# A graph layer on one core: which batches SyncE fetches, how far ahead rows and features are asked for, and where recomputed batches lie

## The chip, the cores and the metric

One core of a Trainium2 chip runs the kernel in one launch. Its engines are TensorE (PE: matmuls; PEld its weight loads), VectorE (DVE), ScalarE (ACT), GpSimd (POOL) and SyncE (SP), which here only issues DMAs. All of it is float32. The metric is device time in microseconds: the median of three runs before is 3925.41 us (3924.81 to 3928.84). A separate profiled execution took 3917.68 us.

## The reference

A layer of a graph network with scalar and vector features on 12500 nodes and 400000 edges, sorted by target node. The number of edges of a node falls along the list, since targets are drawn as 12500 u².

```python
h = relu(layernorm(x))                       # 12500 x 160: 64 scalars, 32 vectors of 3
s = [h0 @ W_sc0, h1 @ W_sc1] * a             # self-connection, a: one number a node
y = [h0 @ W_l1_0, h1 @ W_l1_1] * a           # what a node sends
w = silu(edge_attr_16 @ fc_W1) @ fc_W2       # 192 weights an edge, from 16 features
ys = y[src]                                  # 400000 rows of 160: the gather
mid = products of w, ys and edge_attr_4      # per edge, 96 scalars and 96 vectors
z = zeros.at[dst].add(mid)                   # sum over the edges of a node
out = x + C_S * s + C_X * [z0 @ W_l2_0, z1 @ W_l2_1] * a
```

## The kernel before

**Node stage** (to about 100 us). 98 tiles of 128 nodes are loaded, normalized, transposed and mapped to y, which is stored to a table y_d in HBM, a row of 640 bytes a node. GpSimd uses this time for 72 early fetches of rows of x (L378).

**Edge loop.** The 400000 edges are 3125 tiles of 128, in 782 batches of four tiles. For a batch b the steps are:

- `features` (L393): SyncE loads the edge features, 8 batches in one block `xe`, two DMAs a block.
- `hidden` (L630) and `activate`: TensorE and ScalarE make the hidden layer for two batches.
- `weigh` (L651): the 192 weights of each edge, four matmuls, into `pw`.
- `gather` (L603): GpSimd issues one indirect DMA a tile, 128 rows of y_d into `yg`. Two of a batch's four are issued half a batch later in the loop. An added dependency makes the gathers of batch b + AHEAD wait for the sums of batch b.
- `products` (L561 and L565, the helper `multiply`): VectorE multiplies weights by gathered rows into `pr`; it also makes the selection matrix `sel` (L665, L667).
- `sums` (L681): TensorE multiplies `sel` by `pr` and so adds edges into windows of 32 nodes. A window takes 24 tiles at the start and 3 at the end, four windows are a group; VectorE turns each finished window (L687, L688), and `linear` (L694), `add` (L706) and `accumulate` (L717) bring a group into the output.

Not all batches are gathered by GpSimd:

- **Recomputed batches** (`x_batch`, 18 of them): their rows of x were fetched in the node stage, so y is computed again on the spot. The four rows of a lane lie in slot u of `xr`. The steps are `hot`, `hot_turn` (L776), `look_up` (L788), `pick`, `x_center`, `x_turn` (L803, L804), `x_map` (L816, L817), spread over 16 batches. Before, these batches lie 16 apart: 19, 35, ... 291.
- **Batches that SyncE fetches** (`row_batch`, 12 of them): SyncE reads 16 places from a table `ri` into registers (L618) and issues 16 transfers of one row each (L623), 32 times for a batch. Before, they lie 64 apart: 72, 136, ... 776, and sixteen rows are asked for every two batches. Their rows go into slots of `xr` that are no longer needed.

The **self-connection** is computed in 49 pairs of node tiles (`skip_load` at L727, `skip_turn` L741 and L742, `skip_map` L751 and L752, `skip_add`), a pair every nine batches; before, from batch 296 to 736.

Other work of a block of 24 batches: SyncE loads its four edge numbers, sources and targets (L401, L403, L405) and stores the targets' places in windows (L419), and VectorE computes these (`relate`).

The order is written out by hand: each engine runs its instructions in the order of the Python loop, and waits only for data, for a free buffer or for the added dependencies. `AHEAD = 4`, `EARLY = 8`, `SB = 16` (spacing of recomputed batches), `RB = 64` (spacing of SyncE's batches).

Of the kernel before, what the change touches and what calls it, by code (L numbers as in the profile page):

```python
# [10 lines left out]
F32 = mybir.dt.float32  # L11
# [8 lines left out]
P = 128  # L20
M0 = 64
M1 = 32
D = M0 + 3 * M1
# [6 lines left out]
GT = 4  # L30
# [6 lines left out]
MW = BLK // WTS[-1]  # L37
GN = 8
HN = 2
AHEAD = 4  # L40
EARLY = 8
SB = 16
LATE = 8
XB = 18
SK = 9
RB = 64
RN = 16
LO = D - P
EPS = 1e-5
# [5 lines left out]
def kernel(  # L55
# [19 lines left out]
    nc = tc.nc  # L75
# [47 lines left out]
    GE = NG - LATE  # L123
# [20 lines left out]

    ygp = ctx.enter_context(tc.tile_pool(name="yg", bufs=6))
    ld = ctx.enter_context(tc.tile_pool(name="ld", bufs=2))
    evp = ctx.enter_context(tc.tile_pool(name="ev", bufs=2))
    rp = ctx.enter_context(tc.tile_pool(name="rel", bufs=2))
    RF = RB + 8
    NR = (NB - 1 - RF) // RB + 1  # L150
    RP = 4
    assert NR - 1 <= XB and RP * NR <= P
    ri = const.tile([RP * NR, P // RP * GT], I32, name="ri")
    rg = const.tile([P, GT, D], F32, name="rg")
    blocks, ev4, lows = {}, {}, {}

    before = ctx.enter_context(ExitStack())
# [105 lines left out]
    def row_index():  # L263
        t = row_batch(0) * GT
        for i in range(NR):
            t = row_batch(i) * GT
            nc.sync.dma_start(ri[RP * i:RP * (i + 1), :].rearrange("q (p k) -> q p k", k=GT),
                              src[:, t:t + GT].rearrange("(q p) k -> q p k", q=RP))

    def row_place():  # L270
        nc.vector.tensor_scalar(ri, ri, float(D * 4), None, ALU.mult)
# [86 lines left out]

    def x_batch(u):

        return SB * (u + 1) + 3

    def x_index(us):
        t = x_batch(0) * GT
        every = src[:, t:t + XB * SB * GT].rearrange("p (u r) -> p u r", r=SB * GT)[:, :, 0:GT]
        nc.sync.dma_start(xi[:, us, :], every[:, us, :])

    def x_split():

# [16 lines left out]
    def features(b):  # L386
        blk = b * GT // BT
        if blk not in blocks:

            xe = ld.tile([P, 512], F32, name="xe")  # L390
            v = e16[blk * P:(blk + 1) * P, :].rearrange("(s k f) (h c) -> k s (f h) c", s=4, k=2, h=2)
            for k in range(2):
                nc.sync.dma_start(xe[:, 256 * k:256 * (k + 1)], v[k])  # L393
            blocks[blk] = xe
# [30 lines left out]
    with (  # L425
# [81 lines left out]
        for i, (g, n) in enumerate(groups[:LEAD]):  # L507
            load_x(g, n)
            if i == 1:
                x_index(slice(2, XB))  # L510
                nc.sync.dma_start(a_sb, attr)
        last = len(steps) - 1
        more = list(groups[LEAD:])
# [1 line left out]
        for q in range(len(steps) + 7):  # L515
            if q <= last and steps[q][2] == 0 and more:
                load_x(*more.pop(0))
            for f in range(XB * GT * q // (last + 6), min(XB * GT * (q + 1) // (last + 6), XB * GT)):
                x_fetch(f, mapped.get(q - 6))
            if q == 8:  # L520
                e4_load(0)
            if q == 10:
                row_index()
            for load in loads[2 * q - 24:2 * q - 22] if q >= 12 else []:
                load()
            if q == 24:
                for b in range(min(EARLY, NB)):
                    features(b)
            if q == 16:
                rows_of_windows()  # L530
                lowest(0)
            if q == 18:
                pt = nd_ph.tile([MW, P], F32, name="ph")[:windows_in(0), :]
                turn_low(0, pt)
                most(0, pt)
            if q == 22:
                spread(0, nd_ph.tile([P, MW], F32, name="ph")[:, :windows_in(0)])
            for stage, lag in ((scales, 3), (leave, 7), (out_of_psum, 4), (roots, 2), (turn_rows, 3), (map_rows, 5),
                               (moments, 0), (center, 1)):
                if 0 <= q - lag <= last:  # L540
                    stage(q - lag)
            if q == 2:
                node_weights()
            if q == last + 3:
                nc.vector.tensor_scalar(nm, mv[:, :, 0], -1.0, None, ALU.mult)
                x_split()
                edge_weights()
                relate(rp, 0)
                row_place()
        assert 12 + len(loads) // 2 <= last and x_batch(XB) <= NB  # L550
    before.close()


# [14 lines left out]
    with (  # L568
# [43 lines left out]
        def row_fetch(i, n):  # L612

            b = row_batch(i)
            if n == 0:
                rows[b] = xr[:, i - 1, :, :] if i else rg
            q, o = divmod(n * RN, P // RP * GT)
            _, at_row = nc.values_load_multi_w_load_instructions(  # L618
                ri[RP * i + q:RP * i + q + 1, o:o + RN], engines=[mybir.EngineType.SP], min_val=0, max_val=(N - 1) * D * 4,
                skip_runtime_bounds_check_because="places of nodes, as the indices of the other fetches")  # L620
            for m, v in enumerate(at_row):
                e, k = divmod(n * RN + m, GT)
                nc.sync.dma_start(rows[b].bitcast(U8)[e:e + 1, k, :], y_b[ds(v, D * 4)].unsqueeze(0))  # L623
# [218 lines left out]
        def extras(b):  # L842

            g = group_of[b]
            k = b - first_of[g]
            q, r = divmod(b, KB)
            u, v = divmod(b, SB)
            su, sv = divmod(b - SS, SK)
            if b % 2 == 0 and b + 4 < NB:
                s = (b + 4) // 2  # L850
                activate(s, hidden(s))
            if g and k == 0:
                linear(g - 1)
# [24 lines left out]
            if u < XB and v in (3, 6):  # L878
                left(None)
                picked = look_up(u, HN * (v == 6))  # L880
                waiting[-1] = lambda: pick(u, HN * (v == 6), *picked)
            if r == KB - 6 and q + 2 == NQ:
                left(None)
                cnt = p_x.tile([1, 1], F32, name="px")
                any_far(cnt)
                waiting[-1] = lambda: far_flag(cnt)
            if r == KB - 13 and q + 1 < NQ:
                left(None)
                low_pt = p_x.tile([MW, P], F32, name="px")[:windows_in(q + 1), :]
                turn_low(q + 1, low_pt)  # L890
                waiting[-1] = lambda: most(q + 1, low_pt)
# [12 lines left out]
        for b in range(NB):  # L904
            g = group_of[b]
            k = b - first_of[g]
            if b + EARLY < NB:
                features(b + EARLY)
            q, r = divmod(b, KB)
            if r == 0:  # L910
                e4_load(q + 1)
            if r == KB - 4:
                e4_join(q + 1)
            u, v = divmod(b, SB)
            su, sv = divmod(b - SS, SK)
# [29 lines left out]
        assert SS + NU * SK <= first_of[GE] + K and NQ > 1  # L945
# [162 lines left out]
```

## Time and profile before

| what | before |
|---|---|
| median of three runs | 3925.41 us |
| profiled execution | 3917.68 us, span 3915.5 us |
| busy: TensorE, GpSimd, VectorE, ScalarE | 3586.6, 2917.6, 2748.4, 623.6 us |
| gathers from y_d on GpSimd | 3005, 947 ns each |
| row transfers on SyncE | 6144 |
| mean granted TensorE clock | 0.97 |
| data moved by DMA | 329.82 MB, mean 84 GB/s |

The span runs from the first to the last instruction, and the profiled execution's time holds 2.2 us more. A group of instructions is one line of the code: engine, operation, output<-inputs, count | busy us, mean ns of one | idle us of that engine just before them, and what ended most of it ("issue": nothing that the profile shows). A timeline's row is start, length, engine, line; in brackets the idle time before it. A table of stretches gives for each stretch its length, and the busy time and count of TensorE's matmuls, its weight loads, VectorE, ScalarE and GpSimd, then TensorE's granted clock, the mean share of the DMA engines and GB/s. SPq is SyncE's queue of DMA issues.

### The profile page before, as it was taken

The page shows a single profiled execution, that of the slowest core. Times are in us where ns is not written, and L with a number is a line of the kernel's source. Part 1 is how long each engine was busy: PE and PEld are TensorE (multiplying, and loading weights), DVE is VectorE, ACT ScalarE, POOL GpSimd, SP SyncE. Part 2 cuts the span into 40 slices and gives each one's busy share as a digit, 9 for nine tenths or more (in the row PEclk, how much of TensorE's full clock was granted, in tenths as well). Part 3 has the DMA queues.
Part 4 walks back from the last instruction along what each step waited for, and adds up shares of the span by engine and source line. Part 5 has one row for each costly group of instructions (what it writes and reads, how often), then busy time and mean ns, then how long its engine had stood idle before and what let it go on. Part 6 is the DMA issues. An engine that isn't in the chain of part 4 may idle for free.

```text
span 3915.5 us, 66013 instructions
## 1 busy us (share of the span) xinstructions
PE 3586.6 (92%) x17274; PEld 2321.5 (59%) x17274; DVE 2748.4 (70%) x6899; ACT 623.6 (16%) x1863; POOL 2917.6 (75%) x3085
## 2 busy tenths in 40 slices
PE   7898999999999999889999999989899999999988
PEld 7555555555656655555555565555566666666555
DVE  7566666666667666666677677777677777778776
ACT  6111111111111111111111111111111111111111
POOL 6777777777777777777777777777777777777775
PEclk8899999999999999999999999999999999999999
DMA  8333333323333232333333333333333333333324
GB/s 233 78 79 76 78 78 76 77 73 78 77 75 78 74 80 75 83 83 80 80 82 77 84 79 82 80 80 79 82 80 83 80 79 82 83 80 79 79 74 135
DMA packets 262773, 329.82 MB, mean 84 GB/s; under 512 B 78472, under 2 KB 213160, under 8 KB 262392
## 3 DMA queue, kind: packets, MB, share of 16 engines
q0 software_dynamic: 147696, 252.26, 26.2%
q1 hardware_dynamic: 114072, 73.01, 6.7%
q8 instruction: 140, 2.29, 0.2%
q14 instruction: 241, 1.97, 0.2%
q10 hardware_dynamic: 624, 0.27, 0.0%
HBM read 307.70 MB, written 17.61 MB: 83 GB/s over the span
## 4 chain that ended last, share of the span: by engine, by line
PE 42%; DMA 20%; DVE 18%; issue 11%; POOL 8%; DVEq 1%; SPq 0%; ACT 0%; POOLq 0%; ACTq 0%
PE pz L681 22%; DMA yg<-y_d,src_q 19%; POOL yg L603 8%; PE pw L651 8%; DVE pr L565 7%; PE px L630 5%; DVE pr L561 4%; PE px L694 3%; PE px L706 1%; DVE za L687 1%; DVE at L226 1%; DVE za L688 1%; DVE acc L717 1%; DVE own L665 0%; PE po L485 0%
## 5 line engine op out<-in xcount | busy, mean ns | idle before, releaser
L603 POOL DMA_INDIRECT yg<-y_d,src_q x3005 | 2847.2, 947 | 945.9 <-issue 658.2
L681 PE MATMUL pz<-pr,sel 128*128 128x320 f32 x6250 | 1965.7, 459 | 14.8 <-DVE za L688 14.7
L681 PEld LDWEIGHTS pz<-pr,sel 128*128 128x128 f32 x6250 | 1162.6, 196 | 597.9 <-issue 231.1
L561 DVE TENSOR_TENSOR pr<-pw,yg 128x512 f32<-128x512 f32 x752 | 517.9, 689 | 800.4 <-DMA yg<-y_d,src_q 799.2
L651 PE MATMUL pw<-w,hT 64*128 64x192 f32 x6250 | 737.4, 354 | 252.5 <-DVE pr L565 236.1
L651 PEld LDWEIGHTS pw<-w,hT 64*128 64x128 f32 x6250 | 506.1, 189 | 535.4 <-issue 396.8
L565 DVE TENSOR_TENSOR pr<-pw,yg 128x384 f32<-128x384 f32 x1504 | 760.7, 547 | 0.0
L667 DVE TENSOR_TENSOR sel<-own,pw 128x512 f32<-128x512 f32 x782 | 537.0, 687 | 27.0
L630 PE MATMUL px<-xe,w 32*128 32x512 f32 x782 | 437.3, 640 | 8.8 <-DVE acc L717 7.1
L635 ACT ACTIVATE hT<-px 128x512 f32<-128x512 f32 x391 | 233.4, 597 | 1297.1 <-PE px L630 1292.8
L556 ACT ACTIVATE pw<-ev 128x20 f32<-128x20 f32 x782 | 149.3, 191 | 1417.1 <-PE pw L651 1201.8
L687 DVE STREAM_TRANSPOSE za<-pz 128x160 f32<-128x160 f32 x598 | 203.8, 341 | 233.7 <-PE pz L681 232.8
L694 PEld LDWEIGHTS px<-wo,za 128*128 128x128 f32 x1500 | 211.5, 191 | 106.6 <-issue 68.0
L694 PE MATMUL px<-wo,za 128*128 128x160 f32 x1500 | 243.0, 309 | 8.8 <-DVE high L193 4.3
L630 PEld LDWEIGHTS px<-xe,w 32*128 32x128 f32 x782 | 114.2, 183 | 185.0 <-issue 173.3
L688 DVE STREAM_TRANSPOSE za<-pz 32x160 f32<-32x160 f32 x598 | 201.7, 337 | 20.4
L665 DVE TENSOR_TENSOR own<-iota,pw 128x128 f32<-128x128 f32 x782 | 198.4, 254 | 18.3 <-ACT pw L556 14.7
L706 PE MATMUL px<-os,place 128*128 128x160 f32 x600 | 112.0, 309 | 8.3 <-DVE place L698 3.6
L717 DVE SCALAR_TENSOR_TENSOR acc<-px,a_sb,acc 128x160 f32 x300 | 113.8, 379 | 7.5 <-PE px L706 1.5
L706 PEld LDWEIGHTS px<-os,place 128*128 128x128 f32 x600 | 90.7, 190 | 38.5 <-issue 19.7
L378 POOL DMA_INDIRECT xr<-in_x,xi x72 | 69.2, 962 | 29.2 <-PE po L485 13.7
L696 ACT ACTIVATE os<-px 128x160 f32<-128x160 f32 x150 | 45.6, 304 | 229.6 <-PE px L694 228.6
(131 smaller groups left out, 1380.1 us busy)
## 6 DMA issues: line engine op xcount, KB each, us to landing
xr<-y_d SPq DMA_DIRECT2D x5632, 0.6 KB
yg<-y_d,src_q POOLq DMA_INDIRECT x3005
xe<-in_e SPq DMA_DIRECT2D x196, 128.0 KB
rg<-y_d SPq DMA_DIRECT2D x512, 0.6 KB
xs<-in_x SPq DMA_DIRECT2D x48, 160.0 KB
acc<-in_x SPq DMA_DIRECT2D x11, 640.0 KB
y_d<-ys SPq DMA_DIRECT2D x11, 640.0 KB
out<-acc SPq DMA_DIRECT2D x11, 640.0 KB
```

Source lines behind the costliest of these rows:

```text
L561: nc.vector.tensor_mul(pr[:, :n, :].rearrange("p t (x u) -> p t x u", x=2)[:, :, :, 0:M0], wt[:, :n, 0:NW].rearrange("p t (x u) -> p t x u ...
L565: nc.vector.tensor_mul(pr[:, :n, D * x + M0:D * (x + 1)].rearrange("p t (c u) -> p t c u", c=3), wt[:, :n, 96 * x + M0:96 * (x + 1)].unsqu ...
L603: fetch = nc.gpsimd.indirect_dma_start(out=yg[:, slot(t), :], out_offset=None, in_=y_d, in_offset=bass.IndirectOffsetOnAxis(ap=ev4[t // BL ...
L630: nc.tensor.matmul(ph, w1[r, :], xe[r, :], start=True, stop=True)
L635: nc.scalar.activation(hT, ph, AF.Silu, scale=1.0 / math.sqrt(FC_IN))
L651: nc.tensor.matmul(pw[:, k, 0:NW], hT[r, o:o + P], w2[r, :], start=True, stop=True)
L667: nc.vector.tensor_tensor(sel, own[:, :n, :].unsqueeze(2).to_broadcast([P, n, 4, WN]), wt[:, :n, NW:NW + 4].unsqueeze(3).to_broadcast([P, ...
L681: mm = nc.tensor.matmul(pz[:, 0:PC], sel[:, slot(t), :, :], pr[:, slot(t), :], start=o == 0, stop=last)
L687: nc.vector.transpose(zT[g][:, :, at_w], pz[:, D:PC].rearrange("p (k u) -> p k u", k=ZK))
L688: nc.vector.transpose(zT[g][0:32, :, at_w], pz[0:32, 0:D].rearrange("p (k u) -> p k u", k=ZK))
L694: nc.tensor.matmul(po[:m, :], za[:, k, :m], wo[:, k, :], start=k == 0, stop=k == ZK - 1)
L706: nc.tensor.matmul(ps[:, h, :], place[:m, h, :], os[:m, :], start=True, stop=True)
```

## The change

SyncE's batches become 15, 49 apart (80, 129, ... 766), and sixteen of their rows are asked for every 49 x 16/512 = 1.53 batches, from batch 24 on; each is fully asked for seven batches before its use. They all lie in slots of `xr`, and the separate buffer `rg` goes. Recomputed batches are 43 apart (19, 62, ... 750). Of each 43 batches the first 16 hold the steps of one recomputed batch, and the other 27 hold three pairs of the self-connection, which so runs from batch 16 to about 712. Gathers run six batches ahead of the sums (AHEAD), out of the same six `yg` buffers. Features are asked for 16 batches ahead (EARLY) and have three buffers in a pool of their own. The table of places is loaded at the start of the edge loop (15 loads) and scaled in batch 2, both in the node stage before; the last recomputed batch's index gets a load of its own.

```diff
-AHEAD = 4
-EARLY = 8
+AHEAD = 6
+EARLY = 16
 SB = 16
+PER = 43
...
-RB = 64
+RB = 49
+RS = 24
...
+    fe = ctx.enter_context(tc.tile_pool(name="fe", bufs=3))
...
-    RF = RB + 8
+    RF = RS + RB + 7
     NR = (NB - 1 - RF) // RB + 1
...
-    rg = const.tile([P, GT, D], F32, name="rg")
...
     def x_batch(u):
-        return SB * (u + 1) + 3
+        return PER * u + SB + 3
...
+    def x_index_last():
+        t = x_batch(XB - 1) * GT
+        nc.sync.dma_start(xi[:, XB - 1, :], src[:, t:t + GT])
...
-            xe = ld.tile([P, 512], F32, name="xe")
+            xe = fe.tile([P, 512], F32, name="xe")
...
-            if q == 10:
-                row_index()
...
-                row_place()
...
             if n == 0:
-                rows[b] = xr[:, i - 1, :, :] if i else rg
+                rows[b] = xr[:, i, :, :]
...
-        SS, MAP = SB * XB + 8, 7
+        PAIRS, MAP = (PER - SB) // SK, 7
...
+        def skip_of(b):
+            u, v = divmod(b, PER)
+            if v < SB:
+                return -1, -1
+            return PAIRS * u + (v - SB) // SK, (v - SB) % SK
...
-            u, v = divmod(b, SB)
-            su, sv = divmod(b - SS, SK)
+            u, v = divmod(b, PER)
+            su, sv = skip_of(b)
...
-            if b == SS - 8:
+            if b == SB - 8:
                 skip_load(0)
...
-            if v == 1 and 0 < u <= XB:
-                x_map(u - 1, HN)
+            if v == SB + 1 and u < XB:
+                x_map(u, HN)
...
+            if b == 0:
+                row_index()
...
+            if b == 2:
+                row_place()
-            if v == SB - 2 and u < XB:
+            if v == SB and u < XB:
                 x_scale(u)
...
-            while chunks and chunks[0][0] * RB + chunks[0][1] * RB * RN // (P * GT) <= b:
+            while chunks and RS + chunks[0][0] * RB + chunks[0][1] * RB * RN // (P * GT) <= b:
                 row_fetch(*chunks.pop(0))
```

SyncE's queue early in the edge loop, from one load of a feature block (`xe`) to the next, eight batches later: `TENSOR_LOAD ri` reads sixteen places into registers, and the rows behind it are the transfers of sixteen rows from `y_d`. Before:

```order
64 L393 DMA xe<-in_e 128x1x256 x2
65 L618 TENSOR_LOAD ri
66 L623 DMA rg<-y_d 1x640 x16
67 L618 TENSOR_LOAD ri
68 L623 DMA rg<-y_d 1x640 x16
69 L618 TENSOR_LOAD ri
70 L623 DMA rg<-y_d 1x640 x16
71 L618 TENSOR_LOAD ri
72 L623 DMA rg<-y_d 1x640 x16
73 L393 DMA xe<-in_e 128x1x256 x2
```

and now, with the next feature load as the last row:

```order
79 L622 TENSOR_LOAD ri
80 L627 DMA xr<-y_d 1x640 x16
81 L731 DMA xs<-in_x 128x2x160
82 L622 TENSOR_LOAD ri
83 L627 DMA xr<-y_d 1x640 x16
84 L622 TENSOR_LOAD ri
85 L627 DMA xr<-y_d 1x640 x16
86 L622 TENSOR_LOAD ri
87 L627 DMA xr<-y_d 1x640 x16
88 L622 TENSOR_LOAD ri
89 L627 DMA xr<-y_d 1x640 x16
90 L399 DMA xe<-in_e 128x1x256 x2
```

Five loads of sixteen rows stand between two feature loads instead of four, and among them the load of a pair of node tiles (`xs`), which stood behind batch 288 before.

TensorE's order late in the edge loop, around batch 614 (`px<-wo,za` is `linear` of a group, `pw` the weights of a batch, `pz` its sums, `px<-os,place` is `add`). Before:

```order
2788 L694 MATMUL px<-wo,za 128x160 x5
2789 L651 MATMUL pw<-w_95,hT 128x192 x4
2790 L681 MATMUL pz<-pr,sel 128x320 x4
2791 L198 MATMUL px<-ident,high 128x32
2792 L706 MATMUL px<-os,place 128x160 x2
2793 L651 MATMUL pw<-w_95,hT 128x192 x4
2794 L681 MATMUL pz<-pr,sel 128x320 x4
2795 L630 MATMUL px<-xe,w_94 128x512
```

and now:

```order
2776 L807 MATMUL px<-ident,xr 128x128
2777 L808 MATMUL px<-ident,xr 128x128
2778 L807 MATMUL px<-ident,xr 128x128
2779 L808 MATMUL px<-ident,xr 128x128
2780 L655 MATMUL pw<-w_95,hT 128x192 x4
2781 L685 MATMUL pz<-pr,sel 128x320 x4
2782 L200 MATMUL px<-ident,high 128x32
2783 L820 MATMUL px<-wy_90,sT 128x64
2784 L821 MATMUL px<-wy_91,sT 128x96
2785 L820 MATMUL px<-wy_90,sT 128x64
2786 L821 MATMUL px<-wy_91,sT 128x96
2787 L710 MATMUL px<-os,place 128x160 x2
```

Steps of a recomputed batch (`x_turn` reads `xr`, `x_map` uses `wy`), which all lay before batch 292, now stand here among the sums.

GpSimd's whole order, after its few set-up instructions, is two rows: the 72 early fetches and the gathers. Before:

```order
8 L106 IOTA iota 128x256
9 masks.py:199 AFFINE_SELECT ident<-ident 128x128
10 L109 IOTA lane 128x1
11 L378 DMA xr<-in_x,xi 128x160 x72
12 L603 DMA yg<-y_d,src_q 128x160 x3005
```

and now:

```order
8 L108 IOTA iota 128x256
9 masks.py:199 AFFINE_SELECT ident<-ident 128x128
10 L111 IOTA lane 128x1
11 L384 DMA xr<-in_x,xi 128x160 x72
12 L607 DMA yg<-y_d,src_q 128x160 x2993
```

Twelve gathers are gone, those of three batches of four tiles.

More of the change, by code (lines that the diff above doesn't have):

```diff
@@ L146 @@
     ld = ctx.enter_context(tc.tile_pool(name="ld", bufs=2))
+    fe = ctx.enter_context(tc.tile_pool(name="fe", bufs=3))
     evp = ctx.enter_context(tc.tile_pool(name="ev", bufs=2))
     rp = ctx.enter_context(tc.tile_pool(name="rel", bufs=2))
-    RF = RB + 8
+    RF = RS + RB + 7
     NR = (NB - 1 - RF) // RB + 1
     RP = 4
-    assert NR - 1 <= XB and RP * NR <= P
+    assert NR <= XB and RP * NR <= P and PER < RB
     ri = const.tile([RP * NR, P // RP * GT], I32, name="ri")
-    rg = const.tile([P, GT, D], F32, name="rg")
     blocks, ev4, lows = {}, {}, {}
@@ L359, in x_batch @@
     def x_batch(u):
-        return SB * (u + 1) + 3
+        return PER * u + SB + 3
     def x_index(us):
         t = x_batch(0) * GT
-        every = src[:, t:t + XB * SB * GT].rearrange("p (u r) -> p u r", r=SB * GT)[:, :, 0:GT]
+        every = src[:, t:t + (XB - 1) * PER * GT].rearrange("p (u r) -> p u r", r=PER * GT)[:, :, 0:GT]
         nc.sync.dma_start(xi[:, us, :], every[:, us, :])
+    def x_index_last():
+        t = x_batch(XB - 1) * GT
+        nc.sync.dma_start(xi[:, XB - 1, :], src[:, t:t + GT])
     def x_split():
@@ L509 @@
             if i == 1:
-                x_index(slice(2, XB))
+                x_index(slice(2, XB - 1))
+                x_index_last()
                 nc.sync.dma_start(a_sb, attr)
@@ L548 @@
                 relate(rp, 0)
-                row_place()
-        assert 12 + len(loads) // 2 <= last and x_batch(XB) <= NB
+        assert 12 + len(loads) // 2 <= last and x_batch(XB - 1) < NB - 1
     before.close()
@@ L913 @@
                 e4_join(q + 1)
-            u, v = divmod(b, SB)
-            su, sv = divmod(b - SS, SK)
+            u, v = divmod(b, PER)
+            su, sv = skip_of(b)
             if b + 2 < NB:
@@ L944 @@
             waiting.pop(0)()
-        assert SS + NU * SK <= first_of[GE] + K and NQ > 1
+        assert max(b for b in range(NB) if 0 <= skip_of(b)[0] < NU) <= first_of[GE] + K and NQ > 1
         for h in ([NG - 2] if NG > 1 else []) + [NG - 1]:
```

## The prediction

> **What bounds the kernel now.** I read the page's busy table and slices first, then the costliest groups, then GpSimd's own timeline. TensorE is the busiest engine by its share, but its share is not what to look at.
>
> ```profile
> PE 3586.6 (92%) x17274; PEld 2321.5 (59%) x17274; DVE 2748.4 (70%) x6899; ACT 623.6 (16%) x1863; POOL 2917.6 (75%) x3085
> POOL 6777777777777777777777777777777777777775
> DMA  8333333323333232333333333333333333333324
> L603 POOL DMA_INDIRECT yg<-y_d,src_q x3005 | 2847.2, 947 | 945.9 <-issue 658.2 <-PE pz L681 93.1 <-PE pw L651 38.1
> L561 DVE TENSOR_TENSOR pr<-pw,yg 128x512 f32<-128x512 f32 x752 | 517.9, 689 | 800.4 <-DMA yg<-y_d,src_q 799.2
> ```
>
> VectorE stands idle 799 us in front of the product because the gathered rows have not landed. The 16 DMA engines are about 0.3 busy, so it is not bytes. GpSimd shows the same seven tenths in every slice, which looks like slack until its timeline is read: each gather is busy 0.95 us, and then 0.30 us pass that nothing ends.
>
> ```profile
> 100.48 0.94 POOL L603 DMA_INDIRECT yg<-y_d,src_q  x1 [0.30 <-issue]
> ...
> 2000.40 0.95 POOL L603 DMA_INDIRECT yg<-y_d,src_q  x1 [0.30 <-issue]
> 2001.65 0.95 POOL L603 DMA_INDIRECT yg<-y_d,src_q  x1 [0.30 <-issue]
> ...
> 2012.92 0.94 POOL L603 DMA_INDIRECT yg<-y_d,src_q  x1 [0.30 <-issue]
> ...
> 3892.30 0.95 POOL L603 DMA_INDIRECT yg<-y_d,src_q  x1 [0.30 <-PE pz L681]
> ```
>
> From 2000.40 to 2012.92 ten pitches take 12.52 us: 1.252 us a gather, 5.01 us a batch of four. From the first gather to the last lie 3791.8 us and 3004 pitches; 3004 x 1.252 = 3761.0. So only 30.8 us in the whole edge loop were real waiting: **GpSimd's issue of gathers is the bound from 100 us to 3892 us.** After it comes a tail of 3915.5 - 3892.3 = 23.2 us. A batch that GpSimd does not gather is worth 5.01 us, provided TensorE can take the pace.
>
> Whether it can is read by stage. The columns are the stretch, its length, and busy us (instructions); the second table counts VectorE's `own` and `sel` alone, two instructions a batch, so half its count is the batches.
>
> ```profile
> 101.00:1460.00 1359.00, 1249.43 (x5859) 785.90 (x5858) 898.04 (x2060) 230.62 (x675) 1014.47 (x1071) 0.97 0.31 77
> 1460.00:3180.00 1720.00, 1580.11 (x7484) 1013.71 (x7482) 1217.11 (x3016) 230.10 (x708) 1295.64 (x1369) 0.97 0.32 80
> 3180.00:3680.00 500.00, 470.45 (x2332) 309.28 (x2331) 389.05 (x1003) 70.55 (x218) 376.31 (x398) 0.99 0.32 80
> 3680.00:3894.00 214.00, 196.96 (x950) 128.08 (x948) 164.81 (x428) 27.03 (x88) 160.28 (x170) 0.98 0.40 107
> ...
> 101.00:1460.00 1359.00, 273.32 (x575) 0.97 0.31 77
> 1460.00:3180.00 1720.00, 325.58 (x696) 0.97 0.32 80
> 3180.00:3680.00 500.00, 94.32 (x202) 0.99 0.32 80
> 3680.00:3894.00 214.00, 41.14 (x88) 0.98 0.40 107
> ```
>
> Stage A (to 1460 us, 287.5 batches, all 18 recomputed batches) takes 4.73 us a batch, B (348 batches) 4.94, C (101) 4.95, D (44) 4.86. TensorE is busy 4.35, 4.54, 4.66 and 4.48 us of these.
>
> **The change part by part.**
>
> *Gathers removed.* Fifteen batches instead of twelve go to SyncE, so GpSimd issues 3005 - 12 = 2993 gathers: 12 x 1.252 = **-15.0 us**. Its 72 early fetches are unchanged, so its start at 100.5 us stays.
>
> *Waits of GpSimd removed.* The lead grows from four batches to six, and the 33 batches without a gather are spread evenly: GpSimd's pace becomes 2993 x 1.252 / 782 = 4.79 us a batch everywhere, instead of 4.73 in A and 4.95 behind it. What remains of the 30.8 us depends on TensorE. A recomputed batch costs it these groups:
>
> ```profile
> L788 PE MATMUL px<-look,sT 128*128 128x196 f32 x144 | 31.6, 342 | 0.0
> L817 PE MATMUL px<-wy,sT 128*128 128x96 f32 x144 | 29.8, 288 | 0.0
> L816 PE MATMUL px<-wy,sT 128*128 128x64 f32 x144 | 24.9, 254 | 0.0
> L803 PE MATMUL px<-ident,xr 128*128 128x128 f32 x72 | 18.8, 288 | 2.0 <-DVE acc L717 2.0
> L804 PE MATMUL px<-ident,xr 128*128 128x128 f32 x72 | 18.0, 277 | 0.0
> L776 PE MATMUL px<-ident,oh 128*128 128x128 f32 x72 | 11.8, 286 | 0.0
> L752 PE MATMUL px<-ws,sT 128*128 128x96 f32 x196 | 40.5, 288 | 0.0
> L751 PE MATMUL px<-ws,sT 128*128 128x64 f32 x196 | 34.4, 257 | 1.5 <-DVE acc L717 1.5
> L741 PE MATMUL px<-ident,sh 128*128 128x128 f32 x98 | 25.1, 283 | 4.1 <-ACT hT L635 4.1
> L742 PE MATMUL px<-ident,sh 128*128 128x128 f32 x98 | 24.1, 273 | 0.0
> ```
>
> The first six are 134.9 us for 18 batches, 7.5 us each; the last four are the self-connection, 124.1 us for 49 pairs of node tiles, 2.53 us each. Before, A holds all 18 of the one (0.47 us a batch) and none of the other; B and C hold a pair every 9 batches (0.28). After, every 43 batches hold one recomputed batch (0.174) and three pairs (0.177): 0.351. TensorE's need becomes, A: 4.35 - 0.47 + 0.35 = 4.23; B: 4.54 - 0.275 + 0.35 = 4.62; C: 4.66 - 0.28 + 0.31 = 4.68 (the pairs run out at batch 712); D: at most 4.48 + 7.5/44 = 4.65. How full TensorE can be is seen where it was behind and the rows were there:
>
> ```profile
> 1015.00:1070.00 55.00, 54.76 (x268) 35.33 (x267) 38.61 (x86) 10.18 (x29) 39.92 (x43) 1.00 0.29 71
> 3200.00:3260.00 60.00, 59.01 (x296) 38.47 (x296) 50.74 (x137) 9.03 (x29) 44.81 (x48) 1.00 0.32 80
> ```
>
> 59.01 of 60 is 0.983. The needs divided by that are 4.30, 4.70, 4.77 and 4.73: below GpSimd's 4.79 in every stage, by a tenth in A, where most batches without a gather lay and TensorE's share was already 0.92, and by next to nothing in C. Bounds for the waits left are 0 and today's 30.8 us. I take 12: two in A, the rest for C's tightness, since six batches of lead (29 us) swallow a lag of a few us. Saving **-18.8 us**. VectorE is at 389.05/101 = 3.85 us a batch in C and would have to gain 0.9 us to matter.
>
> *SyncE.* Three more batches are 3 x 512 row transfers with 96 table loads, and they come denser: sixteen every 49 x 16/512 = 1.53 batches instead of every 2. Where SyncE waits for nothing, this is its pace:
>
> ```profile
> 1009.15 0.43 SPq L405 DMA_DIRECT2D dst_q<-in_dst  x1
> 1010.94 25.27 SPq L623 DMA_DIRECT2D xr<-y_d  x64
> 1036.31 1.17 SPq L393 DMA_DIRECT2D xe<-in_e  x2
> ...
> 3433.59 0.40 SPq L727 DMA_DIRECT2D xs<-in_x  x1
> ...
> SPq L419 <- DVE za L687: 293.1, 17, 20.8
> SPq L403 <- DMA yg<-y_d,src_q: 229.1, 73, 8.4
> ```
>
> From 1009.58 to 1036.31, 64 rows with four loads: 6.68 us for sixteen. In 24 batches: 24/1.53 = 15.7 x 6.68 = 104.7 us, three feature blocks (1.17 and the gap behind it) 3.8, the three loads and one store of an edge block, each like the 0.43 of the dst_q row, 1.9, the node tiles of L727 0.8: 111.2 of 24 x 4.79 = 115 us, 97%. Today it is 12 x 6.68 + 6.5 = 86.7 of 24 x 4.94 = 118, and the remainder is waits like those at L419 and L403, where SyncE is ahead of its inputs. Those waits are the cover, and 24 us of every 31 are spent. A chunk is written for seven batches before its use, so SyncE may lag 34 us unseen. I cost it at 0; uncovered it is the slower rival below.
>
> *Smaller edits.* Features 16 batches ahead in a third buffer take their loads out of the risk that SyncE's denser queue brings; today they cost nobody a wait, so 0. The table of places moves from the node stage to the start of the edge loop. Its twelve loads held SyncE from 21.69 us:
>
> ```profile
> 21.69 11.39 SPq L267 DMA_DIRECT2D ri<-in_src  x12
> ...
> L378 POOL DMA_INDIRECT xr<-in_x,xi x72 | 69.2, 962 | 29.2 <-PE po L485 13.7 <-issue 12.5 <-DMA xi<-in_src 1.3
> ...
> 71.81 0.94 POOL L378 DMA_INDIRECT xr<-in_x,xi  x1 [2.22 <-PE po L485]
> ```
>
> Loads of x behind it start 11 us sooner, but GpSimd's 72 early fetches lost only 29.2 - 72 x 0.30 = 7.6 us to waits, the longest of them (2.22) 38 us after these loads: between 0 and -5.4 us, taken 0. At the loop's start fifteen loads at 0.95 hold SyncE for 14 us, and VectorE's scaling of the table, in batch 2, now waits for them: behind it on VectorE stand the products of batch 4, and TensorE waits for those. The few us lie inside GpSimd's lead: 0, and up to +5 without that cover.
>
> *The sum.* 3917.7 (the profiled execution) - 15.0 - 18.8 = 3883.9. The median shown, 3925.4, lies 7.7 above that execution, so **3891 us, 0.9% faster**. With no wait left it is 3880, with all of today's waits 3910.
>
> The Trainium skill says otherwise in DMA: Bandwidth & Descriptors, section "Issuing engines are not separate DMA queues": transfers of all issuing engines share the 16 DMA engines, and a second issuer saves only issue time, "usually small relative to the DMA itself". By that rule the 12 gathers would be worth nothing and the sum 3925. The trace here disagrees: issue is 1.252 us a gather without a break, and the DMA engines are 0.31 busy.
>
> **The rivals.**
>
> *TensorE becomes the bound* in B to D. For it: the needs there are 96 to 98% of GpSimd's pace, and over whole stages TensorE's share never passed 470.45/500 = 0.941. Against it: those stages waited for rows, and the two stretches above held 0.98 and more. At a ceiling of 0.95 B takes 4.86 us, C 4.93, D 4.89 a batch: 24 + 14 + 4 = 42 us over the 3880 without waits, 3922: no change. Under 0.949 it is a loss.
>
> *SyncE falls behind*, the other side. Place: the row transfers of L623; 49 batches last 234.8 us and its other work takes 13, so it decides from 6.92 us for sixteen, 4% over the pace above. At 7.1 us SyncE needs 240.5 us for each fetched batch; the shortfall of 5.7 us uses up the 34 us of margin after six, and nine more each hold VectorE, TensorE and finally GpSimd by 5.7: 51 us on 3891, 3942. For it: 97% full. Against it: 6.68 is measured beside the same gathers, and every wait it has today shrinks first.
>
> *Issue was not the bound*, only latency or shared DMA engines: then moving 12 gathers buys nothing, 3925. Against it stands the unbroken pitch; for it only that VectorE's idle time is booked to the landing.
>
> **How the numbers follow.** A difference under 0.2% (8 us) can't be told from none here. Forecast, GpSimd still the bound at its lower count: 0.72, with 3880 to 3904 as its own range. TensorE the bound: 0.15, half of it faster by a little, a third the same, the rest slower. SyncE behind: 0.07. Issue not the bound: 0.06. Faster: 0.72 + 0.08 = 0.80; same: 0.05 + 0.06 = 0.11; slower: 0.07 + 0.02 = 0.09. The range takes the forecast's with 3 us beneath it for the early loads, and upward the faster part of TensorE's case: 3876 to 3916.
>
> **What would show it.** Right: 2993 gathers at 1.25 us, last start near 3858 us, under 15 us of waits between; about 4.79 us a batch in all stages, so slower than before in A; TensorE's share near 0.88 in A and 0.96 to 0.98 behind; SyncE's waits at L419 mostly gone. Wrong: gathers that wait for `pz` in B and C (TensorE's case); VectorE waiting for `xr` in front of a product (SyncE's case); a gather pitch that moves when SyncE's transfers get denser.

## The result, and the profile after

The changed kernel takes 3876.93 us (median of four runs, 3876.18 to 3880.46); the kernel before takes 3925.11 us (four runs, 3921.35 to 3928.84). The ratio is 0.9879, 95% interval 0.9862 to 0.9896: 48 us faster. The forecast was 3891 in a range from 3876 to 3916, so the sign held, and the time lies 0.9 us inside the range's lower end; it is below the 3880 to 3904 that the prediction gave its forecast as its own range. The profiled execution of the changed kernel took 3877.53 us, its span is 3875.8 us.

In the changed kernel the gather is L607, the product L565, the sums L685, the row transfers of SyncE L627 and the store of places L425. First the page's busy row and its groups for the gather and the product, then GpSimd's timeline, at its first gather, in the middle and at its last:

```profile
PE 3574.7 (92%) x17274; PEld 2318.0 (60%) x17274; DVE 2750.4 (71%) x6899; ACT 622.6 (16%) x1863; POOL 2911.9 (75%) x3073
L607 POOL DMA_INDIRECT yg<-y_d,src_q x2993 | 2841.9, 950 | 913.2 <-issue 649.5 <-PE pz L685 65.9 <-PE pw L655 33.0
L565 DVE TENSOR_TENSOR pr<-pw,yg 128x512 f32<-128x512 f32 x749 | 514.9, 687 | 700.6 <-DMA yg<-y_d,src_q 699.5
...
98.18 0.95 POOL L607 DMA_INDIRECT yg<-y_d,src_q  x1 [0.30 <-issue]
...
2000.66 0.95 POOL L607 DMA_INDIRECT yg<-y_d,src_q  x1 [0.30 <-issue]
2001.91 0.95 POOL L607 DMA_INDIRECT yg<-y_d,src_q  x1 [0.30 <-issue]
...
3852.02 0.95 POOL L607 DMA_INDIRECT yg<-y_d,src_q  x1 [0.30 <-issue]
```

The same work is done by the same engines; what is shorter is the row of gathers. I took every start of a gather from the trace: the pitch is the mean distance of those that follow within 1.3 us, and a wait is what a longer distance has above that pitch. For the kernel before this gives 3004 pitches of 1.2505 us and 35.2 us of waits (the prediction's 30.8 came from the coarser 1.252); after, 2992 pitches of 1.2530 us and 5.0 us of waits. So the span's -39.7 us are the terms below. (Most of the rest of the 48 us is that the profiled execution before lay 7.4 us below the median of its runs; the part on the prediction comes back to that.)

| term | us |
|---|---|
| 12 gathers fewer, 12 x 1.2505 | -15.0 |
| waits between gathers, 35.2 to 5.0 | -30.2 |
| pitch 2.4 ns longer, 2992 times | +7.2 |
| first gather at 98.18 instead of 100.48 | -2.3 |
| tail behind the last start, 23.8 instead of 23.2 | +0.6 |

The waits can be seen in the list of GpSimd's waits. Its columns are the sum in us, the times and the longest; before, then after:

```profile
POOL yg L603 <- PE pz L681: 93.1, 248, 2.3
```

```profile
POOL yg L607 <- PE pz L685: 65.9, 216, 0.3
```

A longest wait of 0.3 us is the idle time that stands before every gather: hardly a gather waits for the sums any more. The stages, with the columns of the prediction's tables (the second time VectorE's `own` alone, one a batch):

```profile
101.00:1460.00 1359.00, 1215.11 (x5583) 758.18 (x5583) 863.84 (x2012) 193.89 (x581) 1028.31 (x1084) 0.96 0.32 80
1460.00:3180.00 1720.00, 1617.10 (x7815) 1046.88 (x7815) 1263.76 (x3108) 260.27 (x788) 1301.91 (x1371) 0.98 0.32 80
3180.00:3680.00 500.00, 485.00 (x2394) 319.42 (x2393) 405.45 (x1035) 79.18 (x242) 378.36 (x399) 0.99 0.31 79
3680.00:3855.00 175.00, 170.06 (x840) 111.35 (x838) 139.16 (x354) 24.30 (x77) 131.11 (x138) 1.00 0.42 115
...
101.00:1460.00 1359.00, 74.19 (x281) 0.96 0.32 80
1460.00:3180.00 1720.00, 88.78 (x358) 0.98 0.32 80
3180.00:3680.00 500.00, 25.63 (x104) 0.99 0.31 79
```

A batch takes 4.84, 4.80 and 4.81 us in A, B and C: even, and slower in A than before (4.73). TensorE is busy 0.894, 0.940, 0.970 and 0.972 of the stages. SyncE's queue, its waits and a stretch of its timeline:

```profile
SPq L425 <- DVE own L669: 33.9, 4, 33.2
SPq L425 <- DVE za L691: 12.0, 6, 3.3
...
2027.48 19.19 SPq L627 DMA_DIRECT2D xr<-y_d  x48
```

The store of places, at which SyncE stood 293.1 and 133.7 us before for the two largest sums, now costs it 33.9 and 12.0, and 33.2 of these are one wait: SyncE reaches the store about when VectorE has the places ready. Its slack is nearly spent, as the prediction said.

### The profile page after: what moved, and what is told of

Its sections match the earlier page's. It is cut to its first block, busy times and chain, and to the rows that moved or that the text cites. A ratio compares the mean times of both kernels' runs of the same rounds, so it can differ in the third digit from the quotient of the medians.

```text
span 3875.8 us, 69190 instructions
## 1 busy us (share of the span) xinstructions
PE 3574.7 (92%) x17274; PEld 2318.0 (60%) x17274; DVE 2750.4 (71%) x6899; ACT 622.6 (16%) x1863; POOL 2911.9 (75%) x3073
## 4 chain that ended last, share of the span: by engine, by line
PE 48%; DMA 17%; DVE 15%; issue 10%; POOL 7%; SPq 1%; DVEq 1%; ACT 0%; POOLq 0%; ACTq 0%
PE pz L685 26%; DMA yg<-y_d,src_q 16%; PE pw L655 10%; POOL yg L607 6%; DVE pr L569 5%; PE px L634 5%; PE px L698 4%; DVE pr L565 4%; PE px L710 1%; SPq L627 1%; DVE at L228 1%; DVE za L691 1%; DVE za L692 1%; DVE acc L721 1%; DMA acc<-in_x 0%
## 5 line engine op out<-in xcount | busy, mean ns | idle before, releaser
L607 POOL DMA_INDIRECT yg<-y_d,src_q x2993 | 2841.9, 950 | 913.2 <-issue 649.5
L685 PE MATMUL pz<-pr,sel 128*128 128x320 f32 x6250 | 1958.6, 458 | 12.5 <-DVE za L692 12.4
L685 PEld LDWEIGHTS pz<-pr,sel 128*128 128x128 f32 x6250 | 1158.8, 195 | 592.0 <-issue 229.8
L565 DVE TENSOR_TENSOR pr<-pw,yg 128x512 f32<-128x512 f32 x749 | 514.9, 687 | 700.6 <-DMA yg<-y_d,src_q 699.5
```

The costliest lines, as they stand in the source:

```text
L565: nc.vector.tensor_mul(pr[:, :n, :].rearrange("p t (x u) -> p t x u", x=2)[:, :, :, 0:M0], wt[:, :n, 0:NW].rearrange("p t (x u) -> p t x u ...
L607: fetch = nc.gpsimd.indirect_dma_start(out=yg[:, slot(t), :], out_offset=None, in_=y_d, in_offset=bass.IndirectOffsetOnAxis(ap=ev4[t // BL ...
L685: mm = nc.tensor.matmul(pz[:, 0:PC], sel[:, slot(t), :, :], pr[:, slot(t), :], start=o == 0, stop=last)
```

## The experiments

The theory at the start was the prediction's: 12 gathers are worth 15 us, and lead and spreading together remove the waits, because an emptier TensorE in the early stage no longer makes GpSimd wait. The rivals were that the lead does it alone, that the spreading does it alone, and that SyncE's denser rows take something back.

One thing has to be known to read the numbers. On three of the chips that these runs met, the kernel before takes 4662 to 4710 us instead of 3914 to 3925, in every run; there each kernel is compared with the kernel before on the same chip. The two kinds of chip are told apart below.

**One part at a time.** Four kernels: the lead alone, the denser rows alone, the spreading alone (with the lead, the early features, the third buffer and SyncE's 12 batches as before), and the whole change with a lead of four.

```diff
--- the kernel before, lead alone
-AHEAD = 4
+AHEAD = 6
--- the kernel before, rows alone
-RB = 64
+RB = 49
--- the changed kernel, spreading alone
-AHEAD = 6
-EARLY = 16
+AHEAD = 4
+EARLY = 8
-RB = 49
-RS = 24
+RB = 64
+RS = 0
--- the changed kernel, lead of four
-AHEAD = 6
+AHEAD = 4
```

> The kernel before with the lead of six batches alone. Theory (GpSimd's issue of 1.252 us a gather sets the end, and a longer lead takes its waits away): still 3005 gathers; the 30.8 us of waits between gathers fall to about 10; 20 us faster, near 3905 us. Rival (the waits come from TensorE's work lying in one stage, the lead is beside the point): waits stay near 30 us and the time at 3925.

> The kernel before with 15 batches for SyncE, 49 apart, alone (sixteen rows every 1.53 batches, features still 8 batches ahead in two buffers). Theory: 2993 gathers, 12 x 1.252 = 15 us less, waits between gathers as before or a little more: 3910 us. Rival (issue is not the bound): 3925. Rival (SyncE can't keep up without the earlier features): VectorE or TensorE waits for rows of xr or for features, slower than 3925.

> The kernel before with the recomputed batches 43 apart and the self-connection between them, alone (12 batches for SyncE 64 apart, lead of four). Theory: still 3005 gathers; most waits lay in the first 1460 us, where TensorE's need falls from 4.35 to 4.23 us a batch while GpSimd's pace slackens from 4.69 to 4.81; waits fall from 30.8 to about 15 us, 3909 us. Rival (the lead removes the waits, the spreading only moves them to the later stages, where TensorE's need rises): 3925 or slower.

> The changed kernel with a lead of four batches again. Theory: 2993 gathers as changed, waits between gathers rise from 8 to about 20 us, 3889 us. Rival (the spreading alone removed the waits): 3877, no difference.

They ran on a chip where the kernel before takes 4663.01 us. Measured: lead alone 4668.60 us, ratio 1.0013 (1.0001 to 1.0025); rows alone 5260.15, 1.1283 (1.1260 to 1.1306); spreading alone 4659.13, 0.9995 (0.9980 to 1.0009); the change with a lead of four 5209.40, 1.1171 (1.1147 to 1.1195). None of the times that the theory expected came on this chip. The busy row of the lead alone on this chip, and of the same kernel on a chip where the kernel before takes 3915 us (last experiment):

```profile
PE 3924.1 (84%) x17274; PEld 2500.3 (53%) x17274; DVE 2737.8 (58%) x6899; ACT 597.9 (13%) x1863; POOL 2923.3 (62%) x3085
```

```profile
PE 3581.0 (92%) x17274; PEld 2318.6 (60%) x17274; DVE 2748.7 (71%) x6899; ACT 622.7 (16%) x1863; POOL 2917.4 (75%) x3085
```

VectorE and GpSimd take the same time for the same instructions, TensorE 343 us more (mean granted clock 0.901 against 0.971). The clock alone does not account for that: in the ScalarE experiment below, on a chip of the ordinary kind, it is 0.880, and TensorE is busy for 3658.3 us. SyncE is hit harder. Of the change with a lead of four, its timeline and, of the whole kernel's waits, one for a late load; then the same for the rows alone:

```profile
2020.87 30.84 SPq L627 DMA_DIRECT2D xr<-y_d  x48
...
DVE sh L738 <- DMA xs<-in_x: 603.1, 30, 36.5
```

```profile
PE px L630 <- DMA xe<-in_e: 610.7, 60, 21.8
```

48 row transfers take 30.84 us, 10.3 for sixteen, where the changed kernel on the other kind of chip, shown above, needs 19.19. That is far over the 6.92 us from which the prediction's SyncE rival decides, and the rival is seen as it was described: VectorE and TensorE wait for loads that stand behind rows in SyncE's queue, 600 us of it. On such a chip 15 batches are too many for SyncE. In the kernels with 12, GpSimd waits for TensorE's sums all along, as in the lead alone:

```profile
POOL yg L603 <- PE pz L681: 387.6, 238, 7.5
```

So these runs tell nothing about what the lead is worth where the gathers are the bound. The spreading alone ran only here.

**The lead of four again, on the other kind of chip.** The same kernel as the fourth above.

> The changed kernel with a lead of four batches, again, since on the chip of the runs ahead of it all engines stalled between instructions and the kernel before took 4663 us. Where the kernel before takes about 3925 us as in the first comparison: theory, waits between gathers rise from 8 to about 20 us, 3889 us (ratio to before 0.991); rival (spreading alone took the waits away): 3877 (0.988). Where it takes about 4660 us again: SyncE needs some 10 us for sixteen rows, so 32 x 10 + 13 = 333 us for each of 15 batches, about 5200 us, whatever the lead.

3920.44 us (10 runs) beside 3914.11 of the kernel before (13 runs): ratio 1.0012 (1.0002 to 1.0022). The theory's 3889 fell: without the lead the change gains nothing, although all 12 gathers are gone (2993 remain) and recomputed batches and pairs are spread. GpSimd's waits and its timeline in the worst place:

```profile
POOL yg L607 <- PE pz L685: 121.4, 237, 5.3
...
3108.36 1.02 POOL L607 DMA_INDIRECT yg<-y_d,src_q  x1 [0.30 <-issue]
3114.68 0.94 POOL L607 DMA_INDIRECT yg<-y_d,src_q  x1 [5.31 <-PE pz L685]
3115.93 0.95 POOL L607 DMA_INDIRECT yg<-y_d,src_q  x1 [0.30 <-issue]
3117.86 0.95 POOL L607 DMA_INDIRECT yg<-y_d,src_q  x1 [0.98 <-PE pz L685]
```

The 12 gathers give 15.0 us and the waits rise from 35.2 to 59.6 us, which takes them back. These waits have a place. I gave each gather its batch and counted the waits by their distance to the last batch that GpSimd does not gather: of the 59.6 us, 54.2 stand in the four batches right behind such a batch, where a sixth of the gathers lie. In the kernel before it is 30.0 of 35.2, in the changed kernel 0.7 of 5.0. One of them in the kernel before, batch 521 behind batch 520, which SyncE fetches:

```profile
2601.05 0.95 POOL L603 DMA_INDIRECT yg<-y_d,src_q  x1 [0.30 <-issue]
2604.34 0.94 POOL L603 DMA_INDIRECT yg<-y_d,src_q  x1 [2.35 <-PE pz L681]
2605.59 0.95 POOL L603 DMA_INDIRECT yg<-y_d,src_q  x1 [0.30 <-issue]
2608.40 0.94 POOL L603 DMA_INDIRECT yg<-y_d,src_q  x1 [1.87 <-PE pz L681]
```

So the new theory: GpSimd jumps over the batch that it does not gather and is then one batch (some 5 us) further ahead of the sums than before. With a lead of four it runs into the added dependency there, and stands until TensorE has caught up. A longer lead should remove these waits. Their number alone does not set their sum: 30 such batches cost 1.0 us each in the kernel before, 33 cost 1.6 each here. In the spread kernel some stand close together (276 and 277, 619 and 621, 664 and 668), and the three pairs hold 17.5 of the 54.2 us; the 5.31 us shown are in front of batch 622. What TensorE's pace has in the rest was not tested apart.

**Three more on a slow chip.** The lead alone again, the change without the spreading (recomputed batches 16 apart and the pairs behind them, as before; lead six and SyncE's 15 batches kept), and the changed kernel with the gathers of 12 more batches left out, whose products use other rows that already lie in `xr`.

```diff
--- the changed kernel, no spreading (core)
-RS = 24
+RS = 28
-        return PER * u + SB + 3
+        return SB * (u + 1) + 3
-            u, v = divmod(b, PER)
-            su, sv = skip_of(b)
+            u, v = divmod(b, SB)
+            su, sv = divmod(b - SS, SK)
--- the changed kernel, 12 batches left out
+            if b in left_out:
+                rows[b] = xr[:, XB - 1, :, :]
+                return
+        left_out = set(range(40, 736, 58)) - xs_of - rows_of
```

> The kernel before with the lead of six alone, where the kernel before takes about 3920 us. Theory, amended by the run ahead of it (GpSimd jumps over a batch that it does not gather, is then one batch further ahead and runs into the limit of its lead; a longer lead takes that away): 3005 gathers, waits between gathers from 31 to under 10 us, 20 to 25 us faster (ratio 0.994). Rival (lead and spreading only work together): waits stay near 30 us, ratio 1.000.

> The changed kernel without the spreading: recomputed batches 16 apart from 19 to 291 and the self-connection behind them, as before; 15 batches for SyncE 49 apart (their asking begins at batch 28 so that none falls on a recomputed one), lead of six, early features. Theory: 2993 gathers, waits of 5 to 15 us, since TensorE's need in the first 1460 us stays under GpSimd's pace: 30 to 40 us faster than before, ratio 0.990 to 0.992. Rival (spreading is what gained): waits of 25 us or more in the first 1460 us, ratio 0.996 or worse.

> The changed kernel with 48 gathers left out: 12 batches, 58 apart from batch 40 on, multiply rows that lie in xr instead of their own, so the output is wrong in them. It takes issue alone away. Theory: 2945 gathers, 48 x 1.252 = 60 us less than the changed kernel if GpSimd still sets the end; TensorE's need of 4.70 to 4.81 against GpSimd's 4.72 takes some back, so 45 to 60 us: 3817 to 3832, ratio to the kernel before 0.972 to 0.977. Rival (TensorE is already the bound): under 20 us, 0.983 or more.

The kernel before took 4662.34 us here. Lead alone 4670.20, ratio 1.0022 (1.0004 to 1.0040); no spreading 5200.74, 1.1160 (1.1130 to 1.1189); 12 left out 5163.41, 1.1087 (1.1046 to 1.1129). The last one has 48 gathers fewer than the change, 60 us of GpSimd's time, and still is 11% slower than the kernel before, 0.7 points below the one without spreading, which differs from it in that too; VectorE waits for SyncE's loads there as above (`xs` 548.7 us). Where SyncE sets the end, leaving gathers out doesn't bring the time back. The lead alone met such a chip a third time:

> The kernel before with the lead of six alone, on a chip where the kernel before takes about 3920 us. Theory (GpSimd jumps over a batch that it does not gather, is then one batch further ahead, and runs into the limit of its lead; a longer lead takes that away): 3005 gathers, waits between gathers from 31 to under 10 us, 20 to 25 us faster, ratio 0.994. Rival (lead and spreading only work together): waits stay near 30 us, ratio 1.000. If the kernel before takes about 4660 us, all engines stall between instructions and the lead does nothing: ratio 1.00.

4725.81 us beside 4710.49, ratio 1.0029 (1.0015 to 1.0044). Nothing for the lead there, rather a little loss; its cause was not followed.

**No spreading, on a chip where the kernel before takes 3922 us.** The kernel without spreading from above.

> The changed kernel without the spreading, on a chip where the kernel before takes about 3920 us: recomputed batches 16 apart and the self-connection behind them, 15 batches for SyncE 49 apart, lead of six, early features. Theory (lead of six takes nearly all waits away, 12 gathers less are worth 15 us, spreading adds little): waits of 5 to 15 us, 30 to 40 us faster, ratio 0.990 to 0.992. Rival (spreading is what gained): waits of 25 us or more before 1460 us, ratio 0.996 or worse. If the kernel before takes about 4660 us, SyncE sets the end as it did there in the earlier runs: about 5200 us.

3877.54 us (3875.73 to 3879.94) beside 3921.87: ratio 0.9882 (0.9866 to 0.9899), the same as the whole change's 0.9879 within the intervals. That is 44 us, a little more than the 30 to 40 expected. The waits are 6.2 us, and GpSimd's longest for the sums again 0.3:

```profile
POOL yg L606 <- PE pz L684: 65.0, 213, 0.3
...
101.00:1460.00 1359.00, 1268.76 (x5980) 800.17 (x5980) 911.04 (x2096) 233.86 (x684) 1028.95 (x1083) 0.97 0.31 78
```

TensorE is busy 0.934 of stage A here, fuller than before (0.919), and GpSimd does not wait. Once the lead is six, the spreading is worth nothing that these intervals would show.

**Going further: nine more batches fetched by ScalarE.** If gathers bound the kernel, 36 fewer are worth 45 us. ScalarE, 16% busy, issues the rows of nine more batches, four at a time between its other work.

```diff
+NA = 9
+AP = 70
+AF0 = 103
+        def act_rows(i, n, h):
+            b = row_batch(i)
+            for m in range(4 * h, 4 * h + 4):
+                e, k = divmod(n * RN + m, GT)
+                nc.scalar.dma_start(rows[b].bitcast(U8)[e:e + 1, k, :], y_b[ds(places[i, n][m], D * 4)].unsqueeze(0))
```

> The changed kernel with nine more batches off GpSimd, 70 apart: ScalarE fetches their rows, four at a time between its activations (sixteen places into registers, then four times four transfers), into slots of xr that are free again. Theory, on a chip where the kernel before takes about 3920 us: 2957 gathers, 36 x 1.252 = 45 us less than the changed kernel, of which TensorE's tight stage takes up to 10 back: 3832 to 3845, ratio to the kernel before 0.977 to 0.981. Rival (TensorE is already the bound, or ScalarE's issues delay the weights' scaling so that VectorE and TensorE wait): under 20 us less, 0.983 or more. If the kernel before takes about 4660 us: SyncE sets the end, near 5200 us.

4717.54 us beside 3918.04: ratio 1.2040 (1.2020 to 1.2061). That is on the side of the rival (0.983 or more), and far beyond it. Its waits:

```profile
ACT pw L563 <- DMA xr<-y_d: 907.0, 343, 18.0
SPq L648 <- DMA xr<-y_d: 861.8, 1009, 80.9
DVE sh L759 <- DMA xs<-in_x: 660.4, 28, 42.2
POOL yg L611 <- PE pz L706: 915.2, 280, 36.7
```

ScalarE and SyncE stand for landings of row transfers before they can go on, SyncE 1009 times. Where one sixteen of SyncE's rows follows another with nothing between, they are 8.80 us apart in the mean instead of the changed kernel's 6.83 (320 places each). SyncE falls behind, and the loads behind its rows are late as on the slow chips, here on a chip of the ordinary kind. That the two queues wait on each other's transfers is read from these waits; what they share was not tested apart.

**The lead alone, on a chip where the kernel before takes 3915 us.**

> The kernel before with a lead of six batches and nothing else of the change (all 3005 gathers stay, third buffer and early fetches left as before). Theory (the lead alone removes the waits of GpSimd, the rest of the gain is the 12 gathers): on a chip where the kernel before takes about 3920 us the waits between gathers fall from about 31-35 us to under 12, and the time falls by 18 to 25 us, ratio 0.9935 to 0.9955. Rival (the waits need the rows fetched by SyncE spread or more of them as well): waits stay above 25 us, ratio 0.998 to 1.001. On a chip where the kernel before takes about 4660 us SyncE and TensorE set the end and the ratio is 1.00 whatever the lead does; then the two are not told apart.

3887.46 us (3886.35 to 3890.83) beside 3914.94: ratio 0.9930 (0.9913 to 0.9946), 27.5 us, a little more than the 18 to 25 expected. All 3005 gathers are there; the waits are 5.2 us, of which 0.2 lie behind the jumped batches. GpSimd's waits and the same gathers of batch 521:

```profile
POOL yg L603 <- PE pz L681: 61.3, 201, 0.3
...
2579.55 0.95 POOL L603 DMA_INDIRECT yg<-y_d,src_q  x1 [0.30 <-issue]
2580.80 0.95 POOL L603 DMA_INDIRECT yg<-y_d,src_q  x1 [0.30 <-issue]
2582.05 0.95 POOL L603 DMA_INDIRECT yg<-y_d,src_q  x1 [0.30 <-issue]
2583.30 0.94 POOL L603 DMA_INDIRECT yg<-y_d,src_q  x1 [0.30 <-DVE own L665]
```

One number at the top of the file gives more than half of the change's gain. The kernels on chips of the ordinary kind, side by side:

| kernel | gathers | pitch us | waits us | last start us | ratio |
|---|---|---|---|---|---|
| before | 3005 | 1.2505 | 35.2 | 3892.30 | 1 |
| lead of six alone | 3005 | 1.2505 | 5.2 | 3860.80 | 0.9930 |
| spread, 15 batches, lead of four | 2993 | 1.2505 | 59.6 | 3897.94 | 1.0012 |
| 15 batches, lead of six, no spreading | 2993 | 1.2527 | 6.2 | 3851.24 | 0.9882 |
| the whole change | 2993 | 1.2530 | 5.0 | 3852.02 | 0.9879 |

The ratios of the second and fourth rows differ by 0.0048, 19 us, for 12 gathers and the early start: 15.0 + 2.2 were the terms for it (first gather at 99.05 and 96.90 us). This fits, but it is no sharp test: each ratio's interval reaches some 7 us either way, and the two times themselves, from two chips and at two pitches, are 9.9 us apart. No run took the 12 gathers away alone on a chip of the ordinary kind.

## Why the prediction was right, and where it was not

- **What bounds the kernel: right.** Gathers set the end before and after. Their count times their pitch, their waits and the two ends make up both spans.
- **Gathers removed, -15.0: right by the accounts**, 12 pitches of 1.2505; the runs fit it, as said, without testing it alone.
- **Waits removed, -18.8: the size was wrong, and so was the step "What remains of the 30.8 us depends on TensorE".** The waits fell by 30.2 us. The prediction let the spreading share in this, because TensorE would be emptier in stage A; without the spreading TensorE is fuller there than before (0.934 against 0.919) and the waits are gone all the same, and with it and a lead of four they grow. They come of the lead's limit, met behind each batch that GpSimd jumps, and with a lead of six they are gone whether TensorE is busy 0.894 or 0.934 of stage A. So the 12 us left, most of them for "C's tightness", had no ground: 5.0 were left, 1.1 of them in C. How long such a wait lasts with a lead of four may still depend on TensorE.
- **SyncE at 97%: right, and the margin thinner than was said.** The estimate of 6.68 us came from one stretch. Over all places where one sixteen follows another with nothing between, the mean is 6.83 us, before (223 places) as after; with 6.92 the point of decision, that is 99%. At 8.80 (with ScalarE's rows) and 9.61 us (the same measure for the lead of four on a slow chip) the rival came true, at several times the 51 us it was priced at. The whole change itself did not run on a slow chip; its two nearest kin lose 11.6 and 11.7% there.
- **Smaller edits at 0:** the first gather came 2.3 us earlier, inside the bounds of 0 and 5.4. Not all of that need be the change's: in the lead alone, whose node stage is as before, it came 1.4 us earlier. The features and the third buffer were not run by themselves.
- **TensorE the bound: did not come true**; its ceiling of 0.95 is passed in C and D (0.970 and 0.972). The forecast share of 0.96 behind A was not reached in B, 0.940.
- **The pitch was taken as fixed.** It was 2.4 ns longer in the run after, 7.2 us in all. A pitch that moves with SyncE's denser transfers was one of the prediction's signs of being wrong, but they did not move it: it is 1.2529 already in the first 80 gathers of the changed kernel, before SyncE's first row transfer at 217 us, and 1.2505 in the lead-of-four kernel with the same rows. Neither the kernel nor the chip alone sets it. The lead alone shows 1.2505 on one chip and 1.2525 and 1.2530 on others, and two kernels on one slow chip (rows alone, lead alone) show 1.2497 and 1.2530. What sets it stays open.
- **The 7.7 us added at the end** were the distance of the profiled execution before from the median; after, that distance is 0.6 the other way. From 3883.9 by the sum, -11.4 for the waits, +7.2, -2.3 and +0.6 make 3878.0, half a us from the profiled execution's 3877.53. The offset and the pitch may be one thing: 2.4 ns on 3004 pitches are 7.2 us. If the kernel before ran at the longer pitch in the comparison, the other four terms (-15.0, -30.2, -2.3, +0.6) make 46.9 of the 48.2 us measured there. It has one trace only, so this is not shown.
- **The range held by 0.9 us, in part by luck.** Of the 14 us by which the forecast was too high, 11.4 are the waits and 2.3 the first gather. The 7.7 us and the longer pitch nearly cancel, which the prediction had no way of knowing.
- **The rule of the Trainium skill** (DMA: Bandwidth & Descriptors, section "Issuing engines are not separate DMA queues") is that a second issuing engine saves only issue time, which is usually small beside the transfer. The prediction took this to make the 12 gathers worth nothing, but the rule leaves them their issue time, and here that time is the bound: 1.25 us a gather without a break, with the DMA engines about 0.32 busy before and after. How long a gather's transfer takes beside that, no view here shows.

## What to carry to other kernels

Where the bound engine skips a piece of its work now and then, it is one piece further ahead right after, so its lead must hold that piece too; look at where its few long waits stand relative to the skipped pieces before you blame the pace of the engine it waits for. An engine that looks idle but only issues transfers has a measurable pace. Take it as a mean over the whole kernel and not from one good stretch, and see how much is left: here it was 1%, and at 8.80 us instead of 6.83 the gain became a loss of 20%. Before you add one execution's distance to a median, trace a second execution: the distance may belong to a term that you take as fixed, as the pitch here.

## What the runs showed of the hardware

- On three of the chips the kernel is slower as a whole; in the lead alone on one of them TensorE needs 3924.1 us instead of 3581.0 for the same instructions and SyncE 10.3 instead of 6.4 us for sixteen of 48 row transfers, while VectorE and GpSimd keep their times. In the same kernel, 27% of the distances between row transfers there lie between 0.6 and 1.2 us, against 2.4% on the other kind. Idle time that nothing in the profile ends grows in that kernel, from 56 us on the other kind to 585 on ScalarE and from 4 to 114 on VectorE. The kernel takes 19% longer; what these chips do differently was not found.
- With rows issued by a second engine, the first one's came slower: 8.80 instead of 6.83 us for sixteen, with 1009 waits of SyncE for landings.
- The pitch of back-to-back gathers on GpSimd differs from one traced execution to another, 1.2497 to 1.2530 us, with no kernel or chip that explains it, and holds from the first 80 gathers to the last.
